# Four fused layers on one core: pools ordered by when they come free, the first attention turns reordered

## The chip, the core and the metric

The kernel runs on one core of a Trainium2 chip. The metric is the device time of one execution in microseconds (us). Engines are named as the profile names them: PE (matrix products and transposes; PEld is its weight load), DVE, ACT and POOL (elementwise work), SP (here the queue that issues transfers). Everything is 32-bit floating point.

## What is computed

A residual stream `x` of 64 sequences of 32 rows of 512 numbers (2048 rows, 16 tiles of 128) passes through four layers. Each layer is a conditional part, chosen per sequence by an index, followed by a feed-forward part, added to `x`:

```python
x = x + _L0_ffn_ref(_L0_cond_ref(x, w0, ids0), ...)          # product with one of 8 matrices; MLP, low-rank path, layer norm
x = x + _L1_ffn_ref(_L1_cond_ref(x, ..., ids1, 0), ...)      # gated MLP with per-sequence rank-16 updates; 8 rank-16 experts
x = x + _L2_ffn_ref(_L2_cond_ref(x, ..., pages, lens), ...)  # attention over 512 cached and 32 own keys; top-2 of 8 experts
x = x + _L3_ffn_ref(_L3_cond_ref(x, ids3, w3), ...)          # mixing of the 32 rows of a sequence; a linear layer
```

In the attention there are 32 query heads on 8 key heads of width 128. Queries and keys get an RMS norm and a rotary turn whose cosine and sine depend on each sequence's length. The cached keys and values lie in pages of 32 positions, 16 pages for each sequence, found through an index.

## The kernel before

The layers run one after the other in one program; `x` goes through memory between them. A scheduler orders each engine's instructions, each engine's queue runs in order, and where the code needs a fixed order on PE (attention and after) `on_pe` chains it. `tc.issue_after(ins)` puts what its block issues on the engine of `ins` behind `ins` in that engine's queue.

On-chip memory is handed out in pools: a pool opened later lies above those still open, from the low end by default, from the high end with `side="right"`. When a layer ends its pools close, and the next layer's pools are laid on the same space. A new pool's first use then waits until every old pool that it lies on has been released as a whole, that is, until the last reader or store of any of its tiles is done. The same holds for the accumulators in PSUM, which each layer fills with pools of its own.

**Layer 0** (`layer0`, L129) takes four groups of four tiles. `products` (L162) multiplies the transposed rows of the group by the chosen matrices: DVE copies four of the eight matrices (`sets`) at a time into `w` (L175), PE multiplies (L179). The products of the next group are stepped through while the current group does its up products (`ph`, L122) and the down products (`pd`, L224). Then follows the layer norm: POOL takes the inverse root (L126), DVE writes `z` from the accumulator (L237) and adds the rows of `x` (L240). ACT issues the store (L241). One pool, `l0_weights`, holds the eight matrices together with all the other weights.

**Layer 1** (`layer1`, L247) takes eight groups of two tiles. `inputs` loads two tiles of `x` and gathers six low-rank matrices by an indirect transfer on POOL (L273). The weights `gate1T`, `up1T` (2752 KB each) and `down1T` are loaded at its start. PE transposes the rows and the gathered matrices (L117, L312), makes the gate and up products (`pg`, `pu`), then `pt`, `pz`, `ph` and `po` (all through L122). DVE makes the output row (L376), ACT issues its store (L377).

**Attention** (`attention`, L421) runs 32 steps: two halves of the heads, 16 tiles each. A step has 16 turns: four sequences times four key heads. In a turn, `scores` (L618) multiplies queries by keys (`sc`, L634) and makes the softmax on DVE and ACT two turns ahead; `turned` transposes the probabilities (`prT_ps`, L484); `values` multiplies them by the values (`po`, L489). The projections of the next step (`pv`, `pk`, four `pq`, L489) are laid in numbered half-turn slots among the turns; the rotary turn of each is made on ACT, DVE and POOL (L521 to L541), and PE transposes the result (`qkT_ps`). Sixteen key pages for a sequence are loaded on SP (L98), the values on POOL (L508).

Ahead of the steps, attention does its setup: small tables, row numbers, and the cosine and sine tables for all tiles (`rotary_tables`, L390). The setup's scratch space is closed before the pool of the weights (`l2_weights`) is opened. Then come the weight loads, the whole first projection, the second tile's rows, the keys and values of the first two sequences, and the first two scores:

```python
        for what in ("v", "k") + GROUPS:
            p.product(what, 0)
            p.product(what, 1)
            if last in ("k",) + GROUPS:
                p.turned(last)
            last = what
        p.turned(last)
```

**The tail** (`Tail`, L817) does the second half of layer 2 and layer 3 for one tile after the other. Its weights take the place of the query weights in the last but one step (`weights`, L842, in slot 17). `run` (L886) loads `y` and `x`, gathers the matrices of layer 3 (L904), and has DVE lay them out as `mix` (L910) in `load`; `choose` makes the routing (L922 to L948), `low_turn`, `low_rank`, `mixed` and `last` follow.

Of the kernel before, what the change touches and what calls it, by code (L numbers as in the profile page):

```python
# [33 lines left out]
P = 128  # L34
# [94 lines left out]
def layer0(c, x_in, x_out):  # L129
# [9 lines left out]
    with ExitStack() as ctx:  # L139
        wp = ctx.enter_context(tc.tile_pool(name="l0_weights", bufs=1))  # L140
        xp = ctx.enter_context(tc.tile_pool(name="l0_x", bufs=2))
        sp = ctx.enter_context(tc.tile_pool(name="l0_seq_weights", bufs=3))
# [4 lines left out]
        def transposed_x(g):  # L147
            return c.load(gp, "xT", [P, KC, N],
                          a["xT"][:, g * N:(g + 1) * N].rearrange("(k p) n -> p k n", p=P))
# [3 lines left out]
        sets = wp.tile([P, KC, n_sets, D], F32, name="sets")  # L153
        for k in range(KC):
            nc.sync.dma_start(sets[:, k], a["cond0T"][:, k * P:(k + 1) * P, :].rearrange("e p o -> p e o"))
        fc1T = c.chunks(wp, "fc1T_0")
        expert = c.chunks(wp, "expert0")
        latent = wp.tile([P, KC, LAT + NE], F32, name="latent")
        nc.sync.dma_start(latent[:, :, LAT:], a["gate0"].rearrange("(k p) n -> p k n", p=P))
        up = c.chunks(wp, "up0")  # L160
# [36 lines left out]
        for g in range(NT // G):  # L197
# [12 lines left out]
            for t in range(G):  # L210
# [30 lines left out]
                nc.scalar.dma_start(x_out(T), z)  # L241
# [5 lines left out]
def layer1(c, x_in, x_out):  # L247
# [5 lines left out]
    with ExitStack() as ctx:  # L253
        wp = ctx.enter_context(tc.tile_pool(name="l1_weights", bufs=1))
        xp = ctx.enter_context(tc.tile_pool(name="l1_x", bufs=4))
        ap = ctx.enter_context(tc.tile_pool(name="l1_gathered", bufs=2))
# [5 lines left out]
        ids = c.load(wp, "ids1", [P, NT // G], a["ids1"], I32)  # L262
        p16 = c.load(wp, "p16", [P, 1], a["p16"])
        rows_f = wp.tile([P, NT // G], F32, name="rows_f")
        nc.vector.tensor_copy(rows_f, ids)
        nc.vector.tensor_scalar(rows_f, rows_f, float(R), p16, ALU.mult, ALU.add)
        rows = wp.tile([P, NT // G], I32, name="rows")
        nc.vector.tensor_copy(rows, rows_f)
        own = c.load(wp, "own1", [P, N], a["own1"])

        def gather(name, g):
            t = ap.tile([P, a[name].shape[1]], F32, name=name)
            nc.gpsimd.indirect_dma_start(  # L273
                out=t, out_offset=None, in_=a[name],
                in_offset=bass.IndirectOffsetOnAxis(ap=rows[:, g:g + 1], axis=0))
            return t

        def inputs(g):
            xs = [c.load(xp, "xt", [P, D], x_in(G * g + t)) for t in range(G)]
            return xs, {n: gather(n, g) for n in ("Ag1", "Au1", "Bg1", "Bu1", "Ad1", "Bd1")}  # L280

        nxt = inputs(0)
        wg, wu = c.chunks(wp, "gate1T"), c.chunks(wp, "up1T")
# [10 lines left out]
        for g in range(NT // G):  # L294
# [50 lines left out]
            for t in range(G):  # L345
# [31 lines left out]
                nc.scalar.dma_start(x_out(G * g + t), o)  # L377
# [43 lines left out]
def attention(c, x_in, y_part, y_out, tail):  # L421
# [13 lines left out]
    with ExitStack() as outer:  # L435
        kp = outer.enter_context(tc.tile_pool(name="l2_const", bufs=1))
        tail.numbers(kp)
        with tc.tile_pool(name="l2_setup", bufs=1) as scratch:
            cos, sin = rotary_tables(c, kp, scratch)

            pages = c.load(scratch, "pages_rows", [P, B * L // P], a["pages_rows"], I32)
            p32 = c.load(scratch, "p32b", [P, 1], a["p32"])
            twice = scratch.tile([P, 1], F32, name="twice")
            nc.vector.tensor_scalar(twice, p32, 2.0, None, ALU.mult)
            rows_f = scratch.tile([P, B * L // P], F32, name="rows_f")
            nc.vector.tensor_copy(rows_f, pages)
            nc.vector.tensor_scalar(rows_f, rows_f, 2.0 * PSIZE, twice, ALU.mult, ALU.add)
            rows = []
            for h in range(HALVES):
                t = kp.tile([P, B * L // P], I32, name=f"v_rows{h}")  # L450
                nc.vector.tensor_scalar(t, rows_f, float(h), None, ALU.add)
                rows.append(t)
            lens_i = c.load(scratch, "lens", [P, B], a["lens"].to_broadcast([P, B]), I32)
            lens = kp.tile([P, B], F32, name="lens_f")
            nc.vector.tensor_copy(lens, lens_i)

            norm = {}
            for n in ("q", "k"):
                w = c.row(kp, n + "_norm")
                ws = kp.tile([P, HD], F32, name=n + "_norm_swapped")  # L460
                nc.vector.tensor_scalar(ws[:, :half], w[:, half:], -1.0, None, ALU.mult)
                nc.vector.tensor_copy(ws[:, half:], w[:, :half])
                norm[n] = (w.rearrange("p (u f) -> p u f", u=2), ws.rearrange("p (u f) -> p u f", u=2))
        keys = c.load(kp, "keys", [P, NK], a["keys"].to_broadcast([P, NK]))
# [8 lines left out]

        wp = outer.enter_context(tc.tile_pool(name="l2_weights", bufs=1))
        ctx = outer.enter_context(ExitStack())
        cp = ctx.enter_context(tc.tile_pool(name="l2_cache", bufs=2))
        qp = ctx.enter_context(tc.tile_pool(name="l2_tile", bufs=2))
        wk = ctx.enter_context(tc.tile_pool(name="l2_work", bufs=1))
        ps = ctx.enter_context(tc.tile_pool(name="l2_psum", bufs=1, space=PSUM))
# [15 lines left out]
        def load_keys(h, b, kT):  # L495
            kt = cp.tile([P, NPP + 1, HKP * PSIZE], F32, name="kt")
            j = b % SEQ
            nc.vector.tensor_copy(kt[:, NPP, :].rearrange("p (g s) -> p g s", g=HKP),
                                  kT[:, :, j * S:(j + 1) * S])
            pages = c.numbers(a["pages"][0:1, b * NPP:(b + 1) * NPP], PAGES)  # L500
            for n in range(NPP):
                c.load_by(kt[:, n, :], a["kT"][ds(pages[n], 1), h].rearrange("a d f -> (a d) f"))
            kts[h, b] = kt
# [24 lines left out]
        def rotated(psrc, tab):  # L528
# [12 lines left out]
            nc.gpsimd.tensor_tensor(r, r, rs.unsqueeze(2).to_broadcast([P, REP, HD]), ALU.mult)  # L541
            return r

        class Projection:
# [6 lines left out]
            def load(self):  # L551
                self.xt = c.load(wk, "xt", [P, D], x_in(self.T))
                self.tabs = {}
                for n in ("q", "k"):
                    ct = qp.tile([P, 2, half], F32, name=n + "_cos")
                    st = qp.tile([P, 2, half], F32, name=n + "_sin")
                    for t, w_n, f in ((ct, norm[n][0], cos), (st, norm[n][1], sin)):
                        nc.gpsimd.tensor_tensor(
                            t, w_n, f[:, self.T, :].unsqueeze(1).to_broadcast([P, 2, half]), ALU.mult)
                    self.tabs[n] = tuple(t.rearrange("p u f -> p (u f)") for t in (ct, st))  # L560

            def x(self):
                pt = transposes("tq", "xT_ps", [self.xt[:, k * P:(k + 1) * P] for k in range(KC)])
                self.xT = wk.tile([P, KC, P], F32, name="xT")
                nc.scalar.copy(self.xT, pt)

            def product(self, what, u):
# [14 lines left out]
                else:  # L582
                    self.r[what] = rotated(self.acc[what], self.tabs[n])
# [86 lines left out]
        def own_part(b, own_prT, oT):  # L670

            po = pos.pop(b)
            for g in range(HKP):
# [4 lines left out]
        ws = {"v": wp.tile([P, KC, HKP * HD], F32, name="wv"),  # L678
              "k": wp.tile([P, KC, HKP * HD], F32, name="wk"),
              "q": wp.tile([P, KC, HQP * HD], F32, name="wq"),  # L680
              "o": wp.tile([P, HQP, D], F32, name="wo")}

# [26 lines left out]
        def keys_of(i):  # L709
            if i < len(turns):  # L710
                s, h, b, _ = of(i)
                load_keys(h, b, projections[s].kT)
# [15 lines left out]

        for what in ("v", "k") + GROUPS:
            weights(0, what)  # L730
        p = projections[0]
        p.load()
        p.x()
        last = None
        for what in ("v", "k") + GROUPS:
            p.product(what, 0)
            p.product(what, 1)
            if last in ("k",) + GROUPS:
                p.turned(last)
            last = what  # L740
        p.turned(last)
        projections[1].load()
        projections[1].x()
        for i in (0, HKP):
            keys_of(i)
            values_of(i)
            own_values_of(i)
        for u in range(HQP // 4):
            output_weights(0, u)
        start(0)  # L750
        start(1)
        oTs, stores = {}, []
        for s, (h, T) in enumerate(steps):
            oTs[s] = qp.tile([P, HQP, P], F32, name="oT")
            slots = [[] for _ in range(2 * per)]
            if s + 1 < len(steps):
# [11 lines left out]
            if s + 2 < len(steps):  # L768
                slots[18].append(projections[s + 2].load)
                slots[28].append(projections[s + 2].x)  # L770
# [4 lines left out]
            if s + 2 == len(steps):  # L775
                slots[17].append(partial(tail.weights, wp))
# [40 lines left out]
class Tail:  # L817
# [5 lines left out]
    def __init__(self, c, x_in, y_in, x_out):  # L823
        self.c, self.x_in, self.y_in, self.x_out = c, x_in, y_in, x_out
# [17 lines left out]
    def weights(self, pool):  # L842

        c, nc, a = self.c, self.c.nc, self.c.a
        room = pool.tile([P, KC, HQP * HD], F32, name="tail_weights", tag="wq") \
            .rearrange("p k n -> p (k n)")
# [13 lines left out]
        self.A3 = chunks("A3", 2, D)  # L860
        self.B3 = pool.tile([P, KC, HKP * HD], F32, name="B3", tag="wv")[:, :2, :]
        nc.sync.dma_start(self.B3, a["B3"].rearrange("(k p) n -> p k n", p=P))
        self.w3 = chunks("W3T", KC, D)
        self.cat = chunks("cat2", KC, self.NE * self.R + self.NE)
        self.base = chunks("base2T", KC, D)
        self.wB = chunks("B2", 1, D)[:, 0, :]
        self.bias = {}
        for n in ("bias2", "bias3"):
            self.bias[n] = place(1, D)[:, 0, :]
            nc.sync.dma_start(self.bias[n], a[n].to_broadcast([P, D]))  # L870
# [15 lines left out]
    def run(self):  # L886
        c, tc, nc, a = self.c, self.c.tc, self.c.nc, self.c.a
        NE, R = self.NE, self.R
        with ExitStack() as ctx:
            tp = ctx.enter_context(tc.tile_pool(name="l3_tile", bufs=2))  # L890
# [225 lines left out]
```

## Time and profile before

| what | value |
|---|---|
| median of 3 runs | 3869.03 us (3868.13 to 3872.56) |
| the profiled execution, its own time | 3868.13 us |
| its span, first to last instruction | 3866.4 us |
| granted PE clock, mean over the span | 0.988 |
| PE busy | 3743.6 us (97%) |
| DVE busy | 1799.8 us (47%) |
| ACT busy | 1300.9 us (34%) |
| POOL busy | 1284.7 us (33%) |
| moved in the execution | 407.46 MB, 105 GB/s on the mean |

How to read it: in the chain of work that ended last PE has 93% of the span. In the list of waits a line names the engine, the operation and its code line, then after the arrow what ended the wait, and last the total in us, the number of times and the longest. In the timeline a line gives the start and the length in us, engine, code line, operation, what it writes and reads, and in brackets the idle time of the engine before it with what ended that. The windows give the busy time of each engine in a stretch, with the number of instructions in brackets.

### The profile page before, as it was taken

What the parts mean: (1) busy time and instruction counts of PE and PEld (TensorE: products, weight loads), DVE (VectorE), ACT (ScalarE), POOL (GpSimd) and SP (SyncE); (2) the same over time, 40 slices, a digit from 0 to 9 for tenths busy, and PEclk for the clock granted to TensorE, in tenths of its full rate; (3) what the DMA queues carried; (4) which work ended last, traced back from release to release, by engine and by line L of the source; (5) the groups of instructions that cost most, each with busy time, mean ns of one, the idle gap of its engine ahead of it and who ended that gap; (6) DMA issues with size and microseconds to landing.
All of it is one profiled execution on the core that took longest, in us unless ns stands there. A gap on an engine that the chain in (4) does not pass through costs nothing.

```text
span 3866.4 us, 60461 instructions
## 1 busy us (share of the span) xinstructions
PE 3743.6 (97%) x17992; PEld 2638.6 (68%) x17992; DVE 1799.8 (47%) x4863; ACT 1300.9 (34%) x3009; POOL 1284.7 (33%) x1289
## 2 busy tenths in 40 slices
PE   6999799999996999999999999999999999999999
PEld 3445688888873777777777777777777777777655
DVE  5432111112124655655565556555655565556433
ACT  0111111111112444444444444444444444444311
POOL 0111200000004544444444444434443454344132
PEclk9999899999997999999999999999999999999999
DMA  5101511111005444344434446544344444444421
GB/s 188 33 22 33 212 44 42 41 44 42 16 11 181 123 121 118 115 115 123 116 112 118 123 140 191 162 149 123 116 120 121 123 118 120 125 119 130 124 77 61
DMA packets 402037, 407.46 MB, mean 105 GB/s; under 512 B 48592, under 2 KB 312784, under 8 KB 401712
## 3 DMA queue, kind: packets, MB, share of 16 engines
q1 hardware_dynamic: 347952, 233.29, 20.1%
q0 software_dynamic: 46848, 157.72, 13.5%
q10 hardware_dynamic: 6912, 12.59, 0.9%
q8 instruction: 147, 2.41, 0.3%
q14 instruction: 178, 1.46, 0.1%
HBM read 382.44 MB, written 20.97 MB: 104 GB/s over the span
## 4 chain that ended last, share of the span: by engine, by line
PE 93%; SPq 1%; DMA 1%; DVE 1%; issue 1%; ACT 1%; DVEq 1%; POOL 1%; POOLq 0%; ACTq 0%
PE po L489 14%; PE sc L634 12%; PE pq L489 11%; PE py L489 11%; PE prT_ps L484 6%; PE pg L122 5%; PE pu L122 5%; PE pz L122 4%; PE po L896 3%; PE ph L122 3%; PE pv L489 3%; PE pk L489 3%; PE pd L224 3%; PE qkT_ps L484 2%; PE pt L122 2%; PE py L179 1%
## 5 line engine op out<-in xcount | busy, mean ns | idle before, releaser
L508 POOL DMA_INDIRECT vt<-in_v_rows,v_rows x512 | 502.4, 981 | 836.4 <-PE po L489 730.9
L489 PEld LDWEIGHTS po<-prT,vt 128*128 128x128 f32 x4096 | 530.6, 192 | 182.9 <-issue 177.6
L639 DVE CUSTOM_DVE_ANT_0 pr<-sc,mask 128x544 f32<-128x544 f32 x512 | 368.9, 720 | 449.5 <-PE sc L634 449.3
L634 PE MATMUL sc<-kt,qT 128*128 128x288 f32 (+1 forms) x2048 | 558.8, 395 | 7.8 <-DMA kt<-in_kT 6.2
L641 ACT ACTIVATE pr<-pr,low 128x544 f32<-128x544 f32 x512 | 383.2, 748 | 504.3 <-DVE low L639 502.3
L489 PE MATMUL po<-prT,vt 128*128 128x128 f32 x4096 | 541.8, 275 | 0.0
L634 PEld LDWEIGHTS sc<-kt,qT 128*128 128x128 f32 x2048 | 370.9, 192 | 185.1 <-issue 111.2
L489 PE MATMUL py<-wo,oT 128*128 128x512 f32 x1024 | 480.3, 592 | 0.8 <-DVE oT L675 0.8
L489 PE MATMUL pq<-wq,xT 128*128 128x512 f32 x1024 | 480.9, 593 | 0.0
L652 ACT COPY prT<-prT_ps 128x512 f32<-128x512 f32 x512 | 298.6, 583 | 419.9 <-PE prT_ps L484 415.1
L646 DVE TENSOR_SCALAR pr<-pr,low 128x512 f32<-128x512 f32 x512 | 310.9, 607 | 16.7
L484 PE MATMUL prT_ps<-ident,pr 128*128 128x128 f32 x2048 | 308.2, 273 | 1.8 <-DVE pr L646 1.8
L489 PEld LDWEIGHTS py<-wo,oT 128*128 128x128 f32 x1024 | 192.0, 190 | 137.8 <-issue 125.7
L489 PEld LDWEIGHTS pq<-wq,xT 128*128 128x128 f32 x1024 | 182.3, 190 | 129.5 <-issue 124.8
L643 DVE RECIPROCAL low<-low 128x1 f32<-128x1 f32 x512 | 83.1, 162 | 346.5 <-ACT pr L641 345.5
L484 PEld LDWEIGHTS prT_ps<-ident,pr 128*128 128x128 f32 x2048 | 241.8, 142 | 2.6 <-issue 2.6
L126 POOL TENSOR_TENSOR rs<-rs,minus_half 128x4 f32<-128x4 f32 x160 | 166.2, 1039 | 195.4 <-DVE rs L524 194.4
L540 POOL TENSOR_TENSOR rot<-rot,swapped 128x512 f32<-128x512 f32 x160 | 202.7, 1267 | 1.0
L644 ACT ACTIVATE own_pr<-pr,low 128x32 f32<-128x32 f32 x512 | 163.9, 320 | 112.5 <-DVE low L643 110.4
L523 DVE TENSOR_REDUCE rs<-squares 128x4 f32<-128x512 f32 x160 | 109.5, 685 | 173.5 <-ACT squares L521 169.6
L541 POOL TENSOR_TENSOR rot<-rot,rs 128x512 f32<-128x512 f32 x160 | 177.4, 1109 | 7.8
L122 PE MATMUL pg<-xT,gate1T 128*128 128x256 f32 (+1 forms) x704 | 170.6, 382 | 0.0
(218 smaller groups left out, 4832.5 us busy)
## 6 DMA issues: line engine op xcount, KB each, us to landing
kt<-in_kT SPq DMA_DIRECT2D x2048, 64.0 KB
xt<-x SPq DMA_DIRECT2D x48, 256.0 KB
wq<-in_WqT SPq DMA_DIRECT2D x12, 1024.0 KB
sets<-in_cond0T SPq DMA_DIRECT2D x4, 2048.0 KB
vt<-in_v_rows,v_rows POOLq DMA_INDIRECT x512, 3.7
wo<-in_WoT SPq DMA_DIRECT2D x8, 1024.0 KB
y<-y SPq DMA_DIRECT2D x32, 256.0 KB
xT<-in_xT SPq DMA_DIRECT2D x4, 1024.0 KB
```

The costliest lines, as they stand in the source:

```text
L122: self.nc.tensor.matmul(out, lhsT, rhs, start=i == 0, stop=i == len(pairs) - 1)
L126: self.nc.gpsimd.tensor_tensor(t, t, self.minus_half[:, :n], ALU.pow)
L484: c.on_pe(nc.tensor.transpose(pt[:, m, :], piece, c.ident))
L489: c.on_pe(nc.tensor.matmul(out, lhsT, rhs, start=first and i == 0, stop=last and i == len(pairs) - 1))
L508: nc.gpsimd.indirect_dma_start(out=vts[b % 2][:, n, :], out_offset=None, in_=a["v_rows"], in_offset=bass.IndirectOffsetOnAxis(ap=rows[h][: ...
L540: nc.gpsimd.tensor_tensor(r, r, tmp, ALU.add)
L541: nc.gpsimd.tensor_tensor(r, r, rs.unsqueeze(2).to_broadcast([P, REP, HD]), ALU.mult)
L634: c.on_pe(nc.tensor.matmul(sc[:, lo + n * PSIZE:lo + m * PSIZE].rearrange("p (n k) -> p n k", k=PSIZE), q, kt[:, n:m, g, :], start=True, s ...
L639: nc.vector.tensor_tensor_reduce(pr[:, :NK], sc[:, lo:lo + NK], masks[h, b], -SCALE, 3.0e38, ALU.add, ALU.min, low[:, 0:1])
L641: nc.scalar.activation(pr[:, :NK], pr[:, :NK], AF.Exp, bias=low[:, 0:1], scale=-1.0, accum_out=low[:, 1:2])
L646: nc.vector.tensor_scalar(pr[:, :L], pr[:, :L], low[:, 2:3], None, ALU.mult)
L652: nc.scalar.copy(prT, pt)
```

## The change

Nothing that is computed changes. Five things do:

1. **Pools.** Layer 0's pool of weights is split. `l0_first` (the eight matrices, `fc1T`, `expert`) is opened first, then the copied matrices, the transposed rows and `up`, then the rest. A pool `known`, opened after layer 0, holds all small tables of layer 1, attention and tail; it and the attention's setup (now `Known`) are issued ahead of layer 1. Layer 1 opens the gathered matrices as two pools, one for even and one for odd groups, then its rows, then gate and up, then the rest. Attention opens its key and value weights, rows and work tiles first, then fixed tiles, query weights, output weights; keys and tiles lie on the right side. The tail's inputs are a right-side pool of their own, the size of the keys' pool.
2. **Queues.** The stores of layers 0 and 1 are issued by SP, no longer by ACT. The gathers of one group are ordered Ag, Au, Ad, Bg, Bu, Bd.
3. **First turns.** The key and value loads of the first two sequences are issued ahead of the first projection, the second sequence's values after it; the first scores start after the third query product, and the last two query transposes move into the slots of step 0. The output weights are queued behind the key pages.
4. **Slots.** The rotary tables of a projection (four POOL operations) move from slot 18 to slot 24. The tail's weights are loaded in five portions in slots 17, 20, 23, 26 and 29.
5. **Tail.** `mix` is made in `low_rank`, no longer in `load`.

The core of the diff:

```diff
-        wp = ctx.enter_context(tc.tile_pool(name="l0_weights", bufs=1))
-        xp = ctx.enter_context(tc.tile_pool(name="l0_x", bufs=2))
+        fp = ctx.enter_context(tc.tile_pool(name="l0_first", bufs=1))
         sp = ctx.enter_context(tc.tile_pool(name="l0_seq_weights", bufs=3))
+        tx = ctx.enter_context(tc.tile_pool(name="l0_transposed_x", bufs=2))
+        up_p = ctx.enter_context(tc.tile_pool(name="l0_up", bufs=1))
+        wp = ctx.enter_context(tc.tile_pool(name="l0_weights", bufs=1))
+        xp = ctx.enter_context(tc.tile_pool(name="l0_x", bufs=2))
...
-                nc.scalar.dma_start(x_out(T), z)
+                nc.sync.dma_start(x_out(T), z)
...
+        aps = [ctx.enter_context(tc.tile_pool(name=f"l1_gathered{i}", bufs=1)) for i in range(2)]
+        xp = ctx.enter_context(tc.tile_pool(name="l1_x", bufs=4))
+        gup = ctx.enter_context(tc.tile_pool(name="l1_gate_up", bufs=1))
         wp = ctx.enter_context(tc.tile_pool(name="l1_weights", bufs=1))
-        xp = ctx.enter_context(tc.tile_pool(name="l1_x", bufs=4))
-        ap = ctx.enter_context(tc.tile_pool(name="l1_gathered", bufs=2))
...
-                nc.scalar.dma_start(x_out(G * g + t), o)
+                nc.sync.dma_start(x_out(G * g + t), o)
...
+        wvk = outer.enter_context(tc.tile_pool(name="l2_key_value_weights", bufs=1))
+        xp = outer.enter_context(tc.tile_pool(name="l2_x", bufs=1))
+        wk = outer.enter_context(tc.tile_pool(name="l2_work", bufs=1))
+        kp = outer.enter_context(tc.tile_pool(name="l2_fixed", bufs=1))
+        wp = outer.enter_context(tc.tile_pool(name="l2_query_weights", bufs=1))
+        op = outer.enter_context(tc.tile_pool(name="l2_output_weights", bufs=1))
+        ctx = outer.enter_context(ExitStack())
+        cp = ctx.enter_context(tc.tile_pool(name="l2_cache", bufs=2, side="right"))
+        qp = ctx.enter_context(tc.tile_pool(name="l2_tile", bufs=2, side="right"))
...
+        with tc.issue_after(p.last_pool):
+            values_of(0)
+        projected("v")
+        for i in (0, HKP):
+            own_values_of(i)
+        projected("k")
+        projected(0)
+        projected(1, "k")
+        projected(2, 0)
+        own_keys(0, 0, p.kT)
+        start(0)
+        projected(3, 1)
+        start(1)
+        with tc.issue_after(p.last_pool):
+            projections[1].tables()
+            values_of(HKP)
         projections[1].load()
         projections[1].x()
...
+        with tc.issue_after(c.last_load):
+            for u in range(HQP // 4):
+                output_weights(0, u)
...
+            if s == 0:
+                slots[0].append(partial(projections[0].turned, 2))
+                slots[2].append(partial(projections[0].turned, 3))
+                slots[2].append(partial(own_keys, 0, 1, projections[0].kT))
...
+                slots[24].append(projections[s + 2].tables)
...
-                slots[17].append(partial(tail.weights, wp))
+                for at, f in zip((17, 20, 23, 26, 29), tail.weights(wp, wvk)):
+                    slots[at].append(f)
...
+            ip = ctx.enter_context(tc.tile_pool(name="l3_in", bufs=2, side="right"))
+            tp = ctx.enter_context(tc.tile_pool(name="l3_tile", bufs=2, side="right"))
...
+            if n != 0 and n == next(m for m in layers if m):
+                kp = ctx.enter_context(tc.tile_pool(name="known", bufs=1))
+                last = Tail(c)
+                last.numbers(kp)
+                known = Known(c, kp)
```

`projected(what, *then)` makes the two halves of one product and then the transposes that are named. `load_keys` now only loads pages; `own_keys` copies the tile's own keys beside them.

## The prediction

> **What bounds the kernel now.** I read the page's first two parts, then PE's waits, then the windows, then the timeline where the waits lie. PE is busy 3743.6 of 3866.4 us, so all that any reordering can bring lies in 122.8 us of PE gaps and in matmuls that run slower just after a gap. The waits of PE:
>
> ```profile
> PE pv L489 <- DMA wv<-in_WvT: 31.0, 1, 31.0
> PE py L179 <- DVE w L175: 30.1, 2, 23.8
> PE qkT_ps L484 <- POOL rot L541: 10.9, 4, 5.8
> PE transposed L117 <- DMA xt<-x: 10.0, 1, 10.0
> PE sc L634 <- DMA kt<-in_kT: 6.2, 3, 2.8
> PE pa L312 <- DMA Ad<-in_Ad,rows: 5.3, 1, 5.3
> ```
>
> See that each is one event or a few, not a steady tax. They lie at the four seams: kernel start (30.1, the first condition weights), layer 0 to 1 (10.0, 5.3), layer 1 to attention (31.0 and the rot waits), and key loads late in attention (6.2). The windows confirm that nothing is to be had between them:
>
> ```profile
> 385.00:430.00 45.00, 24.69 (x82) 16.67 (x81) 6.59 (x18) 6.56 (x12) 18.00 (x19) 0.73 0.67 261
> 430.00:1145.00 715.00, 711.17 (x3285) 592.35 (x3285) 125.95 (x394) 108.57 (x268) 51.47 (x49) 1.00 0.14 43
> 1145.00:1230.00 85.00, 39.50 (x105) 19.60 (x105) 34.17 (x87) 15.52 (x28) 34.21 (x37) 0.74 0.59 193
> 1230.00:3560.00 2330.00, 2328.29 (x12003) 1669.95 (x12002) 1357.50 (x3590) 1051.57 (x2431) 1049.06 (x1059) 1.00 0.43 126
> ```
>
> The second number is PE's busy time, the last three are granted clock, DMA share and GB/s. Layer 1 and attention proper are PE end to end at clock 1.00; the seams have clock 0.73 and 0.74 and heavy DMA. DMA is idle (0.14) all through layer 1, in front of the worst seam: there is room to load early.
>
> The seam into attention, in time order:
>
> ```profile
> 1150.53 0.69 DVE L376 TENSOR_TENSOR o<-po,xt 128x512 f32<-128x512 f32 x1 [2.41 <-PE po L122]
> 1151.27 0.66 PE L484 MATMUL xT_ps<-ident,xt 128*128 128x128 f32 x4 [0.84 <-DVE o L376]
> 1157.45 1.22 DVE L402 TENSOR_TENSOR ang<-pos,freq 128x1024 f32<-128x1024 f32 x1 [1.22 <-DMA freq<-in_freq]
> 1171.55 1.06 ACT L416 ACTIVATE sin<-rest 128x1024 f32<-128x1024 f32 x1 [4.03 <-DVE rest L414]
> 1175.92 0.40 SPq L688 DMA_DIRECT2D wv<-in_WvT  x1
> 1182.95 5.34 PE L489 MATMUL pv<-wv,xT 128*128 128x512 f32 x8 [31.02 <-DMA wv<-in_WvT]
> ```
>
> The weights wait for the whole rotary setup (their space is the setup's), then land 7 us after issue. Also the first transpose starts only when the old layer's last PSUM reader (o) is done: a new pool waits for the whole pool it lies on.
>
> [...] after a 2.77 us gap four transposes took 0.66 us, after 5.78 us 1.11 us. [...] Here the last store was issued at 3863.27 and the span ended at 3866.4, so up to 3.1 us. [...] the moved stores cost 0.33 us of issue each here.
>
> **The change, part by part.** Sums are against the profiled execution, 3868.13 us (span 3866.4 and 1.7 around it); the median 3869.03 is 0.9 above.
>
> *Seam layer 0 to 1.* Size now: the AdT product pt starts at 474.67 in the first group, 1113.16 in the last, so a group takes (1113.16-474.67)/7 = 91.21. From the last pd (395.12) to layer 1's last matmul (1150.44) are 755.3; less 8 x 91.21 = 729.7, the seam costs 25.6. After: the condition sets die with the last copies near 277, so the small tables, both gathered sets and x rows load there; gate and up (2 x 2752 KB, 21 us at the window's 261 GB/s) wait for the last up product at 352 and are in by about 375, 20 us early. Remaining: PSUM comes free when z is read at 397.80 (2.7 us idle); xT lies on layer 0's x pool, free when the last add ends at 399.87, so its copies end about 401 (1.7 idle); the A-transposes' copies lie on layer 0's tile pool, free when the last store has landed, 399.90 + 2 to 3.1. Gate and up products (16 x 0.216 = 3.5 us) can fill that if they are queued there. [...] the residue is 5 to 12; I take 8. **Gain 17.6.**
>
> *Seam layer 1 to attention.* Before, from 1150.44 to the second projection's pv at 1229.87: 79.4. After, I walk PE with rows of this trace: transposes of x at 1151.27 (PSUM again), pv 1.42 later (as 3689.73 to 3691.15) at 1152.7 since wv, wk wait only for the even gathered set (about 1050) and wq for gate and up (about 1107; 6 MB need some 25 us). Four products of 3.43 end at 1166.4. k's rotation needs 6.2 after its product (1191.7 to 1197.87), so 1165.8: in time. Turned k 0.44, product 3.43, turned 0 0.44, 0.7 for the query copy, score 0.92 (1172.3); product 3.43, turned 0.44, 0.7, score 0.92, next x 0.44 (1178.2); prT 0.44, turned 0.44, 0.7, score 0.92: pv at 1180.8, saving 49. Unknown: the cached keys. Their pool lies on layer 1's tile pool, free at the last store's landing, 1151.25 + 3.1 = 1154.3. Sixteen issues at 0.51 (8.09/16) to 0.99 (15.82/16) end at 1162 to 1170, plus 2 to 5 landing: 1164 to 1175 against need at 1171.4, so 0 to 4. POOL adds memsets 1.0, tables 1.8, four gathers at 1.25 (5, or 9 if the first again takes 4.99) before k's rotation, until 1162 to 1166: 0 to 4. I take 3. **Gain 46.**
>
> *Setup moved into layer 0.* Some 20 loads at 0.45 on SP (9 us), about 12 us of DVE, two sines and table loads on ACT (5 us), and 12 gathers at 1.25 (15 us) on POOL, behind PE work of layer 0 that is 99.9% busy. POOL also makes each tile's inverse root; a pd has two buffers and 10.6 us, so a delay under 10 is hidden. Without that cover each gather in front of a root costs 1.25. I take 1 us lost, 0 to 4.
>
> *Stores moved from ACT to SP*, 32 at 0.33: SP is far from full. Behind each is SP's next load, and x rows have two groups of buffers. Nothing.
>
> *Final weights in five slots* instead of one: PE's key waits (6.2) lie 35 to 50 us after that burst. Bytes are the same, so I take 5 of 6.2 (0 to 6.2). Rotary tables six half-turns later: four POOL operations of 0.45, used a step later, nothing.
>
> *Tail.* Before: 3686.64 to the last matmul at 3862.46 is 175.8; sixteen tiles at 10.09 (3710.91 to 3842.13 is 13) are 161.5; loss 14.3:
>
> ```profile
> 3689.73 0.63 PE L918 MATMUL yT_ps<-ident,y 128*128 128x128 f32 x4 [3.08 <-DMA y<-y]
> 3694.14 0.29 DVE L910 TENSOR_TENSOR mix<-sel,own 128x128 f32<-128x128 f32 x1 [1.75 <-DMA sel<-in_cond,rows]
> 3701.88 0.45 PE L961 MATMUL hwT_ps<-ident,hw 128*128 128x128 f32 x1 [3.98 <-DVE hw L948]
> ```
>
> See that y's load and, on DVE, a mix that waits for its gather hold up the routing. After: inputs lie in the keys' space, free after the last score near 3655, and mix comes after routing. Remaining: 0.75 for PSUM, 0.8 for yT, 0.8 for hwT, some 2.5 of drain; residue 5 to 6, 4 to 8 with clock. **Gain 8.5.**
>
> Sum: 17.6 + 46 + 5 + 8.5 - 1 = 76; 3868.1 - 76 = 3792, on the median 3793. With all good ends: 21 + 51 + 6 + 10 = 88 (3781); all bad: 13.6 + 40 + 0 + 6 - 4 = 56 (3813). The start's 30.1 stays. What is late next at each seam is the release of the old pools, no longer a load.
>
> **Rivals.**
> 1. *A new wait takes the loads' place*: keys and POOL gathers queue behind store receipts, and both seams stop again. For: the key pool's place, SP's 15.82 us for one batch, POOL's 4.99 us gather. Against: 7 us of slack. Price: 20 more at attention's start, 10 more at layer 1: 3793 + 30 = 3823.
> 2. *It does not do what it says*: the scheduler puts the early loads into SP's in-order queue behind something that itself waits for the layer's end. Already now a key load stood 35.2 us at SP's head waiting for layer 1's last product. Then only some of the setup's 25 us (1150.6 to 1175.9) comes off: 3869 - 25 = 3844.
> 3. *Slower*: the x stores now sit on SP in front of the next group's x loads. If those loads were queued behind the current group's stores, PE would wait some 10.0 us (the xt row) at each of 10 group boundaries in layers 0 and 1: 3793 + 100 = 3893. It decides from 7.6 us a boundary. Against: four x buffers let a load be queued 91 us ahead, when the group before has been read.
>
> **Chances.** Forecast 0.72 (own range 3781 to 3813), rival 1 0.16, rival 2 0.08, rival 3 0.03, a wash by several small losses 0.01. The range goes from 3778, a little under the good ends, to 3824, the first rival; rivals 2 and 3 stay outside. A measurement here tells 0.2% (8 us) from no change. Faster 0.72 + 0.16 + 0.08 = 0.96, same 0.01, slower 0.03.
>
> **What would show it.** Right: pv's wait for wv gone, pv near 1153 less the first seam's gain; first layer 1 transposes right after z; x transposes released by o; no kt wait after 3560. Wrong: PE waiting for kt or POOL rot above 5 us in attention's start, PE gaps inside layer 0 after 277, or an SP wait of tens of us in front of gate or wq.

## The result and the profile after

The changed kernel takes **3801.1 us**, the median of four runs (3798.88 to 3802.3), where the kernel before takes 3869.03. The ratio is 0.9822 with a 95% interval of 0.9805 to 0.9839: 68 us faster. The forecast was 3793, so 8 us of the expected gain are missing. The profiled execution took 3798.88 us with a span of 3797.0; PE is busy 3732.0 us of it, 98%.

To see where the time went, I cut both spans at the same PE instructions. "Layer 0" runs from the first up product to the last down product; the first seam is the rest up to layer 1's last product less the 729.7 us of eight regular groups; the second seam ends with the second projection's first `pv`; the tail begins at the last 32 output products.

| stretch, us | before | after | gain | forecast |
|---|---|---|---|---|
| start, to the first `ph` | 59.28 | 58.66 | 0.6 | 0 |
| layer 0 | 335.84 | 340.77 | -4.9 | -1 |
| seam layer 0 to 1, beyond 729.7 | 25.62 | 10.63 | 15.0 | 17.6 |
| seam layer 1 to attention | 79.43 | 32.05 | 47.4 | 46 |
| attention | 2442.77 | 2440.76 | 2.0 | 5 |
| tail | 193.76 | 184.43 | 9.3 | 8.5 |
| sum | 3866.4 | 3797.0 | 69.4 | 76 |

Four of PE's waits in the changed kernel, those that the account below needs; the start's 29.5 us, hardly changed, and small ones are left out. The columns are as before (total, times, longest):

```profile
PE ph L122 <- DVE z L241: 4.2, 2, 2.3
PE sc L660 <- DMA kt<-in_kT: 4.1, 3, 3.0
PE transposed L117 <- issue: 2.8, 1, 2.8
PE pt L122 <- ACT AT L118: 2.2, 1, 2.2
```

The waits for `wv` (31.0), for the rows of layer 1 (10.0) and for `Ad` (5.3) are gone, and `rot` has 0.6 left of 10.9. The first line is new: in the kernel before this wait was 0.2 us. The windows at the seams, in the same columns as before:

```profile
385.00:430.00 45.00, 37.32 (x146) 26.32 (x145) 8.72 (x21) 7.20 (x15) 10.33 (x10) 0.92 0.42 148
...
1135.00:1175.00 40.00, 35.32 (x117) 18.22 (x116) 22.28 (x60) 10.69 (x23) 26.82 (x31) 1.00 0.50 157
1175.00:3560.00 2385.00, 2382.85 (x12324) 1712.05 (x12323) 1392.81 (x3683) 1080.18 (x2498) 1076.95 (x1088) 1.00 0.44 129
```

In the 45 us around the first seam PE is now busy 37.32 us, not 24.69, at a clock of 0.92, not 0.73. At the second seam the mean clock is 1.00, before 0.74. That seam in the timeline of the changed kernel:

```profile
1139.86 0.69 DVE L381 TENSOR_TENSOR o<-po,xt 128x512 f32<-128x512 f32 x1 [2.40 <-PE po L122]
1140.61 0.66 PE L504 MATMUL xT_ps<-ident,xt 128*128 128x128 f32 x4 [0.84 <-DVE o L381]
1141.98 3.70 PE L509 MATMUL pv<-wv,xT 128*128 128x512 f32 x8 [0.72 <-ACT xT L591]
...
1161.02 1.18 PE L660 MATMUL sc<-kt,qT 128*128 128x288 f32 x4 [0.73 <-ACT qT L617]
...
1171.81 1.45 PE L509 MATMUL pv<-wv,xT 128*128 128x512 f32 x3
```

PE goes from layer 1's last product to the second tile's `pv` with gaps under a microsecond. The first score waits for its own query copy and not for the key pages. `wv` was issued at 1037.47, 104 us before its use, and `wq` at 1102.09.

### The profile page after: what moved, and what is told of

It is laid out like the page before. It is cut to its first block, busy times and chain, and to the rows that moved or that the text cites. A ratio compares the mean times of both kernels' runs of the same rounds, so it can differ in the third digit from the quotient of the medians.

```text
span 3797.0 us, 60480 instructions
## 1 busy us (share of the span) xinstructions
PE 3732.0 (98%) x17992; PEld 2629.6 (69%) x17992; DVE 1797.3 (47%) x4863; ACT 1299.0 (34%) x3008; POOL 1284.4 (34%) x1289
## 4 chain that ended last, share of the span: by engine, by line
PE 94%; DVE 1%; issue 1%; ACT 1%; SPq 1%; DVEq 1%; DMA 1%; POOL 1%; POOLq 0%; ACTq 0%
PE po L509 15%; PE sc L660 12%; PE py L509 12%; PE pq L509 11%; PE prT_ps L504 6%; PE pg L122 5%; PE pu L122 5%; PE pz L122 4%; PE po L958 3%; PE ph L122 3%; PE pv L509 3%; PE pk L509 3%; PE pd L228 2%; PE qkT_ps L504 2%; PE pt L122 2%; PE py L183 1%
```

## The experiments

**My theory** after the result: the pools and the new order do what the walk said; what is missing was lost in queues. POOL's gathers stand ahead of layer 0's roots, and the last store of layer 0 stands behind a big load on SP. **The rival**: the moved work costs wherever it is queued. The experiments come from several chips, on which the kernel before had medians from 3869.19 to 3874.66, and the same attention code took 2441 us on some and 2447 to 2450 us on others; so I compare stretches within layer 0 and the seams, attention only among runs of one chip, and whole runs by their ratio to the kernel before. Unchanged code varies too: layer 0 took 339.33 to 343.38 us in the eight profiles that have it as in the changed kernel, so a difference of 4 us or less between two single profiles means nothing there by itself; attention took 2446.65 and 2450.49 us in two profiles of the same code on one chip. The seams hardly vary where their code is the changed kernel's: the first took 10.33 to 10.63 us, the second 32.05 in every such run.

### Layer 0: the gathers in POOL's queue

The timeline of the changed kernel at the end of layer 0's third group (start, length, queue or engine, operation, wait):

```profile
313.77 0.46 SPq L85 DMA_DIRECT2D xt<-in_x  x1
315.74 0.94 POOL L278 DMA_INDIRECT Bg<-in_Bg,rows  x1 [0.30 <-issue]
319.13 1.26 POOL L243 TENSOR_TENSOR xt<-xt,beta_row 128x512 f32<-128x512 f32 x1 [2.45 <-DMA xt<-in_x]
...
322.77 0.59 POOL L126 TENSOR_TENSOR rstd<-rstd,minus_half 128x1 f32<-128x1 f32 x1
323.40 0.81 DVE L241 TENSOR_SCALAR z<-pd,mv,rstd 128x512 f32<-128x512 f32 x1 [7.60 <-POOL rstd L126]
324.27 1.12 PE L122 MATMUL ph<-yT,up 128*128 128x512 f32 x2 [1.86 <-DVE z L241]
```

DVE had the variance ready at 315.45. The root came 7.3 us later, because POOL's queue held gathers, and an addition that itself waited 2.45 us for a row. Only then could `z` free the accumulator that `ph` needs.

*gathers_held*: all twelve gathers behind the root of the last group's first tile.

```diff
-        self.nc.gpsimd.tensor_tensor(t, t, self.minus_half[:, :n], ALU.pow)
+        return self.nc.gpsimd.tensor_tensor(t, t, self.minus_half[:, :n], ALU.pow)
...
-                c.inverse_root(rstd, 1)
+                root = c.inverse_root(rstd, 1)
+                if T == NT - G:
+                    c.hold = root.ins
...
-            return xs, {n: gather(n, g) for n in ("Ag1", "Au1", "Ad1", "Bg1", "Bu1", "Bd1")}
+            with tc.issue_after(c.hold):
+                return xs, {n: gather(n, g) for n in ("Ag1", "Au1", "Ad1", "Bg1", "Bu1", "Bd1")}
```

> Held back: layer 1's first twelve gathers are queued on POOL behind the inverse root of the first tile of layer 0's last group, so no gather is issued or moved in layer 0's third group. Theory (gathers, on POOL and on the DMA engines, cost the 4.9 us that layer 0 lost around 315 to 332): the two waits of the up product ph for z (4.2 us) go, layer 0 ends 4 to 5 us earlier (last down product at about 395, not 399.4), total 3797 against the changed kernel's 3801. Rival (the rotary setup on DVE costs it): ph still waits about 4 us for z, total 3801. Second rival: the loss moves to the last group, where the gathers now stand in front of the roots: waits before pd there, total 3801 or more.

Measured: layer 0 took 336.47 us, 4.3 less than in the profile above and below all eight. So the gathers are the cost there and not the setup's loads, DVE or ACT work, which stayed. But the first seam took 14.08 instead of 10.63: now the roots of the last tiles were late, and layer 1's first transposes waited 4.96 us instead of 2.78. The ratio was 0.9822 (0.9805 to 0.9838), just as without the edit: the gain was handed on.

*held_gap* was to put the gathers into POOL's pause of 31 us during the last group's up products. I tied them to the addition of the third group's last tile:

```diff
-                nc.gpsimd.tensor_tensor(xt, xt, beta, ALU.add)
+                added = nc.gpsimd.tensor_tensor(xt, xt, beta, ALU.add)
+                if T == NT - G - 1:
+                    c.hold = added.ins
...
+            with tc.issue_after(c.hold):
```

> The changed kernel, but the twelve first gathers of layer 1 are queued on POOL behind the last row addition of layer 0's third group, where POOL then sits idle for 31 us. Theory (POOL's order alone costs the 4.3 us in layer 0, and the last place tried, behind the first root of the last group, gave them back at the seam because it pushed the last roots): layer 0 falls to 336.5, the seam stays at 10.6, 4 us less than the changed kernel, 0.999 of it. Rival (the gathers' 15 us on POOL and their transfers cost 3 to 4 us wherever they are put): layer 0 and the seam together stay at 350 to 352, no gain.

Measured: a ratio of 0.9834 (0.9821 to 0.9847), beside 0.983 (0.9816 to 0.9843) for the changed kernel run again on that chip; layer 0 took 344.27, the longest of all. Read by its numbers alone, this run speaks for the rival. Its timeline says otherwise: POOL makes that addition two tiles ahead of the root, so the gathers began at 314.72 and lay ahead of the roots of the last two tiles, and one up product waited 5.8 us for `z`. I had put them in the wrong place. The remedy was one more run, *best_pause*, below, which ties them to the scaling (`z` by `gamma`) that follows that tile's root.

### The first seam: whose queue the last store is in

The changed kernel:

```profile
403.49 0.38 SPq L291 DMA_DIRECT2D down1T<-in_down1T  x1
404.22 0.33 SPq L245 DMA_DIRECT2D x<-z  x1
...
416.81 1.07 ACT L118 COPY AT<-transposed 128x512 f32<-128x512 f32 x2 [11.39 <-issue]
```

`AT` lies on layer 0's tile pool and waits for that store to land. It started 12.6 us after the store's issue, and the prediction had given the store 2 to 3.1. The load of `down1T` (2560 KB in this part) was issued 0.7 us ahead on the same queue.

*stores_act* returns the stores of layers 0 and 1 to ACT:

```diff
-                nc.sync.dma_start(x_out(T), z)
+                nc.scalar.dma_start(x_out(T), z)
...
-                nc.sync.dma_start(x_out(G * g + t), o)
+                nc.scalar.dma_start(x_out(G * g + t), o)
```

> The stores of layers 0 and 1 go back to ACT's queue, all else as in the changed kernel. Theory (the last store of layer 0, issued on SP 0.7 us after layer 1's 2.5 MB weight load, lands late because it stands behind that load in the same queue, and holds the copies of the transposed A matrices for 12 us): the copy AT comes 3 to 5 us after the store's issue in place of 12.6, and PE's 2.2 us wait for it goes; the seam costs 8, not 10.6 us. Rival ([...] the receipt is late anyway): AT still 10 us or more after the store.

```profile
403.29 0.33 ACTq L245 DMA_DIRECT2D x<-z  x1
...
410.33 1.07 ACT L118 COPY AT<-transposed 128x512 f32<-128x512 f32 x2 [5.38 <-issue]
```

*store_first* keeps SP and queues `down1T` and the small weights behind the last store:

```diff
+                c.stored = nc.sync.dma_start(x_out(T), z).ins
...
+        with tc.issue_after(c.stored):
+            nc.sync.dma_start(wd[:, :full, :], a["down1T"][:full * P].rearrange("(k p) n -> p k n", p=P))
...
```

> Layer 1's down-projection and later weights are queued on SP behind layer 0's last store, which stays on SP. Theory (order within SP's queue decides when the store lands): AT is copied 3 to 4 us after the store's issue, PE waits under 1 us for it, the seam costs about 8 us, total 3798 to 3799 against 3801. Rival (the store is slow for another reason): AT still about 12 us late, and as the queue was laid out for an early one, PE waits longer, up to 9 us more.

```profile
404.84 0.33 SPq L245 DMA_DIRECT2D x<-z  x1
...
407.15 1.07 ACT L118 COPY AT<-transposed 128x512 f32<-128x512 f32 x2 [1.11 <-DMA x<-z]
```

Only here does the profile name the store as what released the copy; in the two others it names nothing. In *stores_act* the trace still shows it: the 256 KB of ACT's queue moved from 407.96 to 409.81, just ahead of the copy at 410.33. In the changed kernel the store's packets can't be told from the load's, but those of `cat`, two places behind the store in the same queue, have a size of their own and begin at 414.57.

From the store's issue to the copy: 12.6 us behind `down1T` in the same queue (12.2 to 12.6 in the nine runs with this order), 7.0 from another queue beside `down1T` (one run), 2.3 with the load queued behind it (2.3 to 2.5 in three runs). So *store_first* bears its theory out; *stores_act* lies between its theory (3 to 5) and its rival (10 or more). The store's place in the queue made most of the difference. How the load delays a store on another queue was not shown; why the store on ACT's queue moved its first packet only 4.7 us after its issue (403.29 to 407.96) stays open.

In time the gain is smaller, since gate and up products fill the wait: the seam took 7.21 us with the store first (-3.4), and 11.74 with the store on ACT, where only four matmuls of those products stood ahead of `pt` (32 in the changed kernel) and it waited 2.78 us. The totals were 3805.72 us (one run) for *stores_act* and a ratio of 0.9818 (0.9801 to 0.9834) for *store_first*: only the stretch resolves them.

### The second seam: early loads or the new order

*old_order* keeps all pools and early loads, and gives the first projection and first turns their old order (the loop quoted in the section on the kernel before, with the two query transposes taken out of step 0's slots).

```diff
-        projected("k")
-        projected(0)
-        projected(1, "k")
-        projected(2, 0)
-        own_keys(0, 0, p.kT)
-        start(0)
-        projected(3, 1)
-        start(1)
...
+        for what in ("v", "k") + GROUPS:
+            p.product(what, 0)
+            p.product(what, 1)
+            if last in ("k",) + GROUPS:
+                p.turned(last)
+            last = what
...
```

> The order of the first attention turns is undone, the pools and early loads stay: all six products first, each transposed one product later, the scores after all of them, no transposes in step 0's slots. Theory (the early loads bring most of the 47 us, the order only spares waits for the rotary turn): PE waits for rot return with 6 to 11 us, and a first softmax of 3 us is uncovered, so the stretch from layer 1's last product to the second projection's pv takes 42 to 46 us in place of 32.0. Rival (the order brings half of it): 50 us or more. Rival (order brings nothing): 33 us.

Measured: the seam took 44.9 us, 12.9 more, within the theory's 42 to 46; the run (one) took 3820.71 us. In PE's waits the old one is back:

```profile
PE qkT_ps L504 <- POOL rot L564: 9.0, 3, 5.2
```

*late_weights* keeps the order and issues `wv`, `wk` and `wq` behind layer 1's last store:

```diff
+                c.stored = nc.sync.dma_start(x_out(G * g + t), o).ins
...
+        with tc.issue_after(c.stored):
+            for what in ("v", "k") + GROUPS:
+                weights(0, what)
```

> The changed kernel, but the attention's first weights (wv, wk, wq: 6 MB) are issued behind layer 1's last store, as they were before; pools, order of the first turns and setup stay new. Theory (early loading is the larger part of the 47 us at this seam): pv waits 5 to 8 us for wv, the key pages queue behind 6 MB on the same queue and the first scores wait some 10 more, so the stretch from layer 1's end to the second projection grows from 32.1 to 47 to 55 us, the run 15 to 23 us longer. Rival (the setup in the way was the cost, the loads would have been hidden behind the first products): only pv's first wait, plus 5 to 8 us.

Measured: 53.11 us, 21.1 more, and 3826.2 us for the run (one). The size is the theory's, but by luck, since the steps are not: `wv` cost 5.08 us, the scores did not wait for keys, and the largest wait is this one (SP's line, then PE's):

```profile
1153.91 33.59 SPq L98 DMA_DIRECT2D kt<-in_kT  x32
1187.60 0.37 SPq L85 DMA_DIRECT2D xt<-x  x1
...
1193.34 1.09 PE L504 MATMUL xT_ps<-ident,xt 128*128 128x128 f32 x4 [13.11 <-DMA xt<-x]
```

The second tile's row stands in SP's queue behind 32 key pages here. In the changed kernel it stands ahead of them:

```profile
1141.29 0.32 SPq L85 DMA_DIRECT2D xt<-x  x1
1142.79 23.84 SPq L98 DMA_DIRECT2D kt<-in_kT  x32
```

So the edit did more than it was meant to: the order of SP's queue changed with it, in this run alone, and the issue of the pages took 33.59 us, not 23.84. The row's 13.1 us are a cost of that order and not of late weights as such. What is left, 8.0 us, is the rival's size (5 to 8), so this run does not show that early loading is the larger part. If the parts add up, the seam's 47.4 us are 12.9 of order, 8.0 of early weights and 26.5 for the setup that no longer stands there. The last was not tried alone; it fits the trace before, where `wv` was issued at 1175.92, behind the setup and 25.5 us after layer 1's last product (1150.44).

### The end of attention and the tail

*tail_at_once* loads all five portions of the final weights in slot 17, as before; *outputs_early* lays the last step's output products in half-turns 3, 5, ... 17. Both ran on one chip, with *late_weights* and *tail_late*, whose attention is the changed kernel's (2441.94 and 2442.55 us).

```diff
-                for at, f in zip((17, 20, 23, 26, 29), tail.weights(wp, wvk)):
+                for at, f in zip((17, 17, 17, 17, 17), tail.weights(wp, wvk)):
```

> The changed kernel, but all five portions of the final weights in half-turn 17 as before. Prediction's step (the burst makes the keys late, 5 of 6.2 us): key waits in the last steps grow from 3.6 to 6 to 9 us, attention 3 to 5 us longer than in the other runs beside it. Rival (the short turns of the last step make them late): attention at most 2 us longer.

```diff
-                for u, at in enumerate((18, 19, 21, 23, 25, 27, 29, 31)):
+                for u, at in enumerate((18, 19, 21, 23, 25, 27, 29, 31) if s + 1 < len(steps)
+                                       else (3, 5, 7, 9, 11, 13, 15, 17)):
```

> The changed kernel, but in the last step the eight output products lie in half-turns 3, 5, ..., 17 instead of 18 to 31, so that its first turns are no longer the shortest of all. Theory (the 3.6 us of key waits left at 3564 come from turns of 2.43 us against 16 key issues of 0.5 to 0.8 us): the early wait falls to 0 to 1, attention 2 to 3 us shorter. Rival 1 (keys are late whatever the turns' length, since the issue waits for the buffer): unchanged. Rival 2: the wait moves to the second half of the step, where the turns have become short, and attention is the same or longer.

The waits for keys, first with the weights at once, then with the outputs early:

```profile
PE sc L660 <- DMA kt<-in_kT: 5.2, 3, 3.5
```

```profile
PE sc L660 <- DMA kt<-in_kT: 0.8, 1, 0.8
```

With all weights at once attention took 2441.65 us, no more than the two runs beside it, whose key waits were 5.6 and 4.8. Spreading the weights brought nothing that can be seen. With the outputs early (one run) it took 2435.48 us, 6.2 to 7.1 less, more than the 2 to 3 expected; the key waits account for 4.0 to 4.8 of that, and the rest was not traced. The key waits came from the last step itself: it has no projections, so its first turns were 2.43 us each, and four of them (9.7 us) don't cover the issue of 16 pages plus their landing: in the changed kernel 10.2 us, from the first issue (3555.58) to the last score that waited for them (3565.80).

*tail_late* opens the pool of the tail's inputs after that of its tiles, so that it doesn't have the keys' space for itself:

```diff
-            ip = ctx.enter_context(tc.tile_pool(name="l3_in", bufs=2, side="right"))
             tp = ctx.enter_context(tc.tile_pool(name="l3_tile", bufs=2, side="right"))
+            ip = ctx.enter_context(tc.tile_pool(name="l3_in", bufs=2, side="right"))
```

> The changed kernel, but the pool of the tail's inputs is opened after that of its tiles, so that it no longer lies on the keys' space alone. Theory (the tail's gain is its inputs' early space): yT waits about 3 us for y again as before, the first gather comes late, tail 184.4 to 188 to 190 us. Rival (the gain is that mix no longer stands ahead of the routing on DVE): the tail stays within 1 us of 184.4.

```profile
PE yT_ps L975 <- DMA y<-y: 3.0, 1, 3.0
...
PE hwT_ps L1018 <- DVE hw L1005: 1.9, 1, 1.9
```

The tail took 191.78 us, 7.35 more, beyond the 188 to 190 expected; in all other runs of the new tail it took 184.4. So the inputs' space is most of the 9.3 us of gain. What is left, 2.0 us, fits the later place of `mix`, which was not tried alone.

### The three remedies together

*best* joins *held_gap*, *store_first* and *outputs_early*; *best_pause* is the same with the gathers tied to the scaling:

```diff
+                scaled = nc.gpsimd.tensor_tensor(z, z, gamma, ALU.mult)
+                if T == NT - G - 1:
+                    c.hold = scaled.ins
```

> The changed kernel itself once more, to stand beside the next two. Both theories: 0.982 to 0.983 of the kernel before, layer 0 340.8, first seam 10.6, attention 2441.

> The changed kernel with the gathers in POOL's pause, the later weights of layer 1 queued behind layer 0's last store, and the last step's output products early. If the three costs are separate: 4.3 + 3.4 + 5.3 = 13 us less than the changed kernel, 0.9966 of it (3788 beside 3801), 0.979 of the kernel before. If they share a cause or one wait takes the place of another: 5 to 8 us less.

> As the kernel called best, but the twelve gathers are queued on POOL behind the last scaling of layer 0's third group (the operation after that group's last root), not behind an addition that POOL makes two tiles earlier. In the queue they then stand between the roots of the third group's last tile and the fourth group's first, with one addition among them. Theory (only a gather ahead of a root costs): layer 0 falls from 342.5 to 336.5 and no wait of the up products for z over 0.5 us is left; the first seam stays at 7.2; 6 us less than best: 0.9795 of the kernel before. Rival (the gathers or their transfers cost wherever they lie): layer 0 stays above 340.

| run | layer 0 | first seam | attention | median, us | ratio to before, 95% |
|---|---|---|---|---|---|
| after_again | 339.33 | 10.51 | 2450.49 | 3807.22 | 0.983, 0.9816 to 0.9843 |
| best | 342.54 | 7.15 | 2441.27 | 3799.69 | 0.981, 0.9797 to 0.9824 |
| best_pause | 336.47 | 6.53 | 2442.17 | 3793.58 | 0.9793, 0.978 to 0.9806 |

*best* gave 7.5 us of the 13. Its gathers lay as wrongly as in *held_gap*, ahead of two roots, and an up product waited 3.6 us for `z`: layer 0's 342.54 us lie within the spread of the unchanged code, and the 4.3 us hoped for there did not come. POOL's queue in *best_pause*:

```profile
327.56 0.55 POOL L126 TENSOR_TENSOR rstd<-rstd,minus_half 128x1 f32<-128x1 f32 x1 [2.57 <-DVE rstd L238]
...
330.48 1.58 POOL L280 DMA_INDIRECT Ag<-in_Ag,rows  x1 [0.18 <-issue]
...
346.01 0.95 POOL L280 DMA_INDIRECT Bd<-in_Bd,rows  x1 [0.30 <-issue]
366.08 0.57 POOL L126 TENSOR_TENSOR rstd<-rstd,minus_half 128x1 f32<-128x1 f32 x1 [19.12 <-DVE routed_by L223]
```

All twelve gathers lie between two roots, with 19.12 us to spare. Layer 0 takes 336.47 us, as the theory said to the tenth, the seam stays short, and of PE's waits for `z` one of 0.2 us is left. So the rival falls: the same gathers cost nothing where no root stands behind them. The move takes their transfers away from the third group's rows as well, and these had a share: over all runs with the stores on SP, a row that an addition waited for was used 2.6 to 3.2 us after its issue with no gather beside it, and 3.4 to 6.9 us (14 loads) with gathers. How much of the cost was POOL's queue and how much the slower rows was not separated. Beside the kernel before, *best_pause* is 81 us faster. It did not run beside the changed kernel; the ratios, 0.9793 against 0.9822 and 0.983, put it 11 to 14 us below that.

## Why the prediction was right, and where it was off

- **Second seam (46, measured 47.4): right, by its own steps.** The walk gave 30.4 us, the measured stretch is 32.05. Each landmark came as walked: transposes released by `o`, `pv` 1.4 us later, scores without a wait for keys. Of the 3 us allowed for the unknown keys and gathers, 1.65 were used, and not by them: from a query's transposes to its score it took 1.33, 1.33 and 1.61 us, walked 1.14, a score 1.02, not 0.92, and PE waited 0.33 for the copy of the second tile's rows, which the walk had left out. The gathers came every 1.25 us, as priced, and the one of 4.99 did not come back.
- **First seam (17.6, measured 15.0): mechanism right, one term mis-sized.** Transposes right after `z`, with 2.78 us idle (walked 2.7), came true. "Free when the last store has landed, 2 to 3.1" failed: it was 12.6, because the stores were moved into the queue in which `down1T` stood. The 2 fits the trace before, where this store, issued on ACT at 399.90, moved its last packet by 401.93, 2.0 us later; it is near the 2.3 of *store_first*. In both the big loads were issued behind the store. I had priced that move at 0.33 us of issue each. That is not enough here: the queue decided between 2.3, 7.0 and 12.6 us. Gate and up products hid most of it, as the walk also said, so 3.4 us came of it. The residue of 8 was my estimate; it was 10.63. No run undoes the early loads here: that they bring the 15.0 is read from the waits for rows and `Ad` that are gone, not tried.
- **Setup moved into layer 0 (1 lost, measured 4.9): the cover failed.** "A delay under 10 is hidden" by the two buffers of `pd` was the step. At the end of a group the next user is not a `pd` 10 us later but the `ph` that takes the same buffers at once, and besides gathers an addition that waited for its row stood ahead of the root. The bound I gave, 0 to 4, was too narrow, too: the eight profiles with this layer 0 give 3.5 to 7.5. PE gaps inside layer 0 after 277 were one of the signs of being wrong that the prediction named, and this one came.
- **Final weights in five slots (5, measured 2.0): the step was wrong in its cause.** The burst does not make the keys late; the short turns of the last step do. The sign "no kt wait after 3560" did not come: 3.6 us of key waits stand there. The 2.0 us in the profiled pair match the fall of the key waits from 6.2 to 4.1, but are luck as far as the runs show: the key waits of all ten runs of the new attention that keep the output products late lie between 3.0 and 7.0 us.
- **Tail (8.5, measured 9.3): right**, and mostly for the first of its two reasons (7.35 us of it).
- **Rivals.** The first, new waits behind the landing of stores, happened on a small scale at the first seam (3.4 us where it had 10) and not at the second. The second did not happen: `wv` was on its way 104 us early. The third did not happen in the changed kernel, since SP has each store ready when it comes to it; but *late_weights* shows its mechanism at work, a row load behind other entries of SP's queue: 13.1 us.

The missing 6.6 us of the sum are then 3.9 in layer 0, 2.6 at the first seam and 3.0 in attention, less 1.4 at the second seam, 0.8 in the tail and 0.6 at the start (6.7; rounding).

## What to carry to other kernels

When work is moved early, check each in-order queue that it is moved into, and ask what stands behind it there: twelve gathers of 1 us each, some of them ahead of tiny roots, cost more than all the setup's other moves (4.3 us of layer 0's 4.9). An experiment's edit can reorder a queue, too, as *late_weights* did, so the queue of each run has to be looked at before its time is read. Tie such work to the last operation of a phase after which the engine pauses (layer 0 took 336.47 us in *best_pause*, 344.27 in *held_gap*), and look at the queue itself, since the order in the source is not the order in the queue. A small transfer on which a pool's release hangs belongs ahead of big loads in its queue (2.3 us to the copy that waits for it, beside 12.6 behind the load); and where waits for loads stand in the last of many equal steps, first ask what that step lacks.

## What was not expected of the hardware

- From the issue of one 256 KB store to the copy that waits for it to land: 2.3 to 2.5 us on SP with a load of 2560 KB queued behind it (three runs), 7.0 us on ACT beside that load on SP (one run), 12.2 to 12.6 us on SP behind the load (nine runs).
- In layer 0, a 256 KB row load on SP was used 2.6 to 3.2 us after its issue with no gather beside it (326.72 to 329.34 in the changed kernel) and 3.4 to 6.9 us with gathers beside it (5.4 there, 313.77 to 319.13).
- The issue of 32 key pages took SP 23.84 us in the changed kernel and 33.59 us in *late_weights*, where 6 MB of weights had been issued just ahead of them (from 1146.05 on).
